# The tail between attention and the GELU stage rewritten: weight matrices on GpSimd's queue, some input rows loaded early, eight larger convolution steps

## The chip, the cores and the metric

The kernel runs on one core of one Trainium2 chip. The metric is the device time of one execution in microseconds (us), as a median of several runs. A profiled execution gives the trace, in which times are counted from the start of its span.

## What is computed

Two layers on an image batch of shape (4, 128, 128, 128): four images, 128 channels, 128 by 128 pixels, all in float32.

```python
# layer 0: windowed attention, then a feed-forward part with a 5x5 depthwise convolution
reg = windows of 16x16 pixels, step 14, so 9x9 per image        # neighbours share 2 rows/columns
tok = out_proj(attention(layernorm(reg))) + reg                 # 4 heads of 32
xf  = overlap-mean of the windows, back to the image
y   = layernorm(xf) @ w_p0 + b_p0                               # 128 -> 256 channels
ym  = depthwise_conv_5x5(y)                                     # 256 channels
ym  = batchnorm over (image, row, column) of ym
y   = gelu(gelu(ym)) @ w_p2 + b_p2 + xf
# layer 1: quantise to 4 bits, conv3x3, batchnorm, quantise, conv3x3, batchnorm, + identity
```

Two points matter here. The batch norm after the 5x5 convolution needs the mean and variance of every image, so no GELU can run before the last piece of the convolution is done. And a row of the convolution's output needs two rows of its input above and below it.

## The kernel before

**Bands.** Attention works in bands: `bands` lists 4 images times 9 rows of windows, 36 in all. In step t of the main loop the attention of band t runs, beside the layer norm of the bands to come, the post-processing of band t-1 and pieces of the convolution of bands long done. `beside(t)` returns these side steps and `run` carries them out; the order on TensorE, ScalarE, VectorE and SyncE is the order written in the program (`manual_schedule`). Each `normalise` ends in `spread`: a row of reciprocal deviations, stored by ScalarE's queue into `row`, is read back to all partitions as `xn`. Post-processing (`post_begin`, `post_chunks`) forms the seams of `ob` on GpSimd, multiplies with `wo` (L510), stores `xf`, normalises, multiplies with `wp0` (`p0`, L526; its result `y` is copied by ScalarE at L531) and stores `y` to `y2_d` in DRAM. A band's last `p0` steps are kept in the list `left` and run one band later.

**Convolution.** `y2_d` holds, per image, rows with two rows of padding above and below, columns split into even and odd. The convolution takes 16 output rows (`GR`) at a time: 20 input rows times two column parities are the 40 rows of the contraction (`KD`). For each channel a 40x32 matrix, three of them for the column shifts, is multiplied with 64 columns of each of `ng` row groups. Two channel halves and four channels run side by side in TensorE. The matrices lie in `dw_d`, built in the first band. `units` lists the pieces of the whole work: three whole images, then the last image in three parts: groups 0 to 3, groups 4 and 5, groups 6 and 7. The last part, `units[-1]`, reads rows up to the image's end and so can only be finished after the last band.

**The tail before.** After the main loop the band pools close (`bctx.close()`). Two pools are opened in their place (`tail`), with one buffer for the matrices and four for the rest. SyncE's queue issues the loads of the first four of eight matrix tiles `all_w`; then `run(beside(T))` does the last `left` steps and the post-processing of band 35; then `conv_steps(len(units) - 1, 4, ...)` runs sixteen steps of 8 channels a half. A step loads one input tile `u` four steps ahead (four DMAs: two halves, rows 0 to 15 and 16 to 19, 2 KB contiguous), multiplies (L611) into two `sc` tiles of PSUM in turn, copies both halves with ScalarE (L618), takes `bn_stats` on VectorE (L622), and puts four stores of 64 KB to `cv_d` on ScalarE's queue, in pieces of 256 bytes. The other four matrix tiles are loaded by SyncE's queue in the first four steps.

**After it.** 64 `bn_aggr` (L973), two small matmuls (L985) and `affine` (L913 to L919) give scale and shift. `gelu_stage` loads `cv` and `xfl` (L1099, L1104) and starts with image 0.

All DMAs of SyncE and ScalarE take turns on eight completion semaphores; each DMA waits until the one that used its semaphore before has landed.

Of the kernel before, what the change touches and what calls it, by code (L numbers as in the profile page):

```python
# [8 lines left out]
F32 = mybir.dt.float32  # L9
# [5 lines left out]
P = 128  # L15
# [5 lines left out]
NT = RS * RS  # L21
# [10 lines left out]
GR = 16  # L32
CW = P // 2
KD = 2 * (GR + 4)
NCK = 8
# [11 lines left out]
def layers(  # L47
# [127 lines left out]
    with ExitStack() as actx:  # L175
# [1 line left out]
            tc.tile_pool(name=f"{name}_{tag}", bufs=bufs, **k)  # L177
        )
        rp, op = pool("rp", 2), pool("op", 2)
        y2p, up, cp = pool("y2p", 1), pool("up", 3), pool("cp", 2)  # L180
        work, dev, xnp, xfp = pool("work", 1), pool("dev", 2), pool("xnp", 3), pool("xfp", 2)
        rowp = pool("rowp", 4, space=bass.MemoryType.DRAM)
        small = pool("small", 6)
# [3 lines left out]
        bctx = actx.enter_context(ExitStack())  # L187
        pool = lambda name, bufs: bctx.enter_context(tc.tile_pool(name=f"{name}_{tag}", bufs=bufs))
        xp, yp, sums = pool("xp", 2), pool("yp", 2), pool("sums", 1)
        att, attn_t, attn_v = pool("att", 2 if safe else 4), pool("attn_t", 2), pool("attn_v", 2)  # L190


# [203 lines left out]
        def flush(n, engine=nc.sync):  # L396
            for out, in_ in stores[:n]:
                engine.dma_start(out=out, in_=in_)
            del stores[:n]
# [149 lines left out]
        def weights(wt, k, jj, n, dma):  # L549
            for half in range(2):  # L550
                dma(
                    out=wt[64 * half : 64 * half + KD].rearrange("p s c m -> p s (c m)"),
                    in_=dw_d[2 * k + half, :, :, 256 * jj : 256 * (jj + n)],
                )

        def conv_steps(n, ahead=2, rest=None):

            b, g0, ng = units[n]  # L560
            nc_ = min(8, 32 // ng)
            tiles = [(k, jj, c) for k in range(NCK) for jj in range(2) for c in range(0, 8, nc_)]
            steps, U, W = [], {}, {}
            nj = nc_ // 4

            def load(at):
                k, jj, c = tiles[at]
                if rest:
                    W[k, jj] = rest[0][k][:, :, 8 * jj : 8 * jj + 8, :]
                    ut = rest[1].tile([P, ng * nc_ * CW], F32, name="u")  # L570
                else:
                    if c == 0:
                        W[k, jj] = up.tile([P, 3, 8, 32], F32, name="w")
                        weights(W[k, jj], k, jj, 1, nc.sync.dma_start)
                    ut = up.tile([P, 32 * CW], F32, name="u")[:, : ng * nc_ * CW]
                U[at] = ut = ut.rearrange("p (g c x) -> p g c x", g=ng, c=nc_)
                for half in range(2):
                    ch = 32 * k + 16 * half + 8 * jj + c
                    for a, z in ((0, GR), (GR, GR + 4)):
                        nc.sync.dma_start(  # L580
                            out=ut[64 * half + 2 * a : 64 * half + 2 * z].rearrange(
                                "p g c x -> p g (c x)"
                            ),
                            in_=bass.AP(
                                y2_d[b].tensor,
                                y2_d[b][GR * g0 + a, 0, ch, 0:1].offset,
                                [[2 * P * CW, 2 * (z - a)], [GR * 2 * 2 * P * CW, ng], [1, nc_ * CW]],
                            ),
                        )

            def products(at):
                k, jj, c0 = tiles[at]
                ut, wt = U.pop(at), W[k, jj]
                if rest:
                    sc = ps_s.tile([P, 2, 2, NT], F32, name=f"sc{at % 2}")
                    pc = [
                        sc[:, half].rearrange("p a n -> p (a n)")[:, : nj * ng * CW].rearrange(
                            "p (j g x) -> p j g x", j=nj, g=ng
                        )
                        for half in range(2)  # L600
                    ]
                else:
                    pc = [ps_m.tile([P, nj, ng, CW], F32, name="pm") for _ in range(2)]
                for j in range(nj):

                    for s, (a, z) in ((1, (0, CW)), (0, (1, CW)), (2, (0, CW - 1))):
                        for half in range(2):
                            hs = slice(64 * half, 64 * half + KD)
                            for q in range(4):
                                c = 4 * j + q  # L610
                                nc.tensor.matmul(  # L611
                                    pc[half][32 * q : 32 * q + 32, j, :, a:z],
                                    wt[hs, s, c0 + c, :], ut[hs, :, c, a + s - 1 : z + s - 1],
                                    start=(s == 1), stop=(s == 2),
                                )
                for half in range(2):
                    cv = (rest[1] if rest else cp).tile([P, nj, ng, CW], F32, name=f"c{half}")
                    nc.scalar.copy(  # L618
                        cv.rearrange("p j g x -> p (j g x)"), pc[half].rearrange("p j g x -> p (j g x)")
                    )  # L620
                    for j in range(nj):
                        nc.vector.bn_stats(  # L622
                            st0[:, k, half, 2 * jj + c0 // 4 + j, n, :], cv[:, j].rearrange("p g x -> p (g x)")
                        )
                        ch = 32 * k + 16 * half + 8 * jj + c0 + 4 * j
                        store(
                            bass.AP(
                                cv_d[b].tensor,
                                cv_d[b][g0, ch, 0:1].offset,
                                [[CW, P], [2 * P * GR * P, ng], [1, CW]],  # L630
                            ),
                            cv[:, j],
                        )

            def begin():
                for at in range(ahead):
                    load(at)

            steps.append(begin)
            for at in range(len(tiles)):  # L640
                def one(at=at):
                    if at + ahead < len(tiles):
                        load(at + ahead)
                    products(at)

                steps.append(one)
            return steps

        def attention(t):

# [199 lines left out]

        T = len(bands)
        todo, share, left, early = [], [0], [], []
        wq, kscale, tail = [], [], []
        one, two = quantised(0, w1), quantised(1, w2)
        for n in range(len(one) + 1):
            todo += one[n : n + 1] + two[max(n - 1, 0) : n]
# [10 lines left out]
        with nullcontext() if safe else tc.manual_schedule(engines=MANUAL):  # L867
            ln1_begin(0)
            for steps in zip(*ln1_chunks(0)):
                run(steps)  # L870
            last = None
            for t in range(T):
                flush(len(stores))
                scores, halves, values_in, values = attention(t)
                if t + 1 < T:
                    ln1_begin(t + 1)
                for j, side in enumerate(beside(t)):
                    scores(j)
                    if last:
                        last()  # L880
                    run(side[0])
                    halves(j)
                    if j == 0 and t:
                        post_begin(t - 1)
                    run(side[1])
                    if j % 2 == 0:
                        values_in(j)
                    run(side[2])
                    run(side[3])
                    last = lambda j=j, values=values: values(j)  # L890
            last()
            post_begin(T - 1)
            flush(len(stores))

            bctx.close()
            tail += [actx.enter_context(tc.tile_pool(name=f"late{n}_{tag}", bufs=n)) for n in (1, 4)]
            all_w = [tail[0].tile([P, 3, 16, 32], F32, name=f"w{k}") for k in range(NCK)]
            for k in range(NCK // 2):
                weights(all_w[k], k, 0, 2, nc.sync.dma_start)
            run(beside(T))  # L900
            flush(len(stores))
            run(todo)
            for n, s in enumerate(conv_steps(len(units) - 1, 4, (all_w, tail[1]))):
                s()
                flush(len(stores), nc.scalar)
                if n < NCK // 2:
                    weights(all_w[NCK // 2 + n], NCK // 2 + n, 0, 2, nc.sync.dma_start)
            flush(len(stores))

    def affine(mean, var, n, gamma, beta, name):  # L910

# [378 lines left out]
```

## Time and profile before

| | |
|---|---|
| median of 3 runs | 3295.52 us (3294.91 to 3316.36) |
| the profiled execution | 3291.11 us |
| its span | 3289.0 us |
| TensorE busy | 3093.5 us (94%) |
| VectorE, ScalarE, GpSimd busy | 2020.6 us, 1992.0 us, 828.3 us |
| DMA moved | 682.76 MB, mean 208 GB/s |
| DMA packets | 812363, of these under 512 bytes 581646 |

The span is what the profiler saw between first and last instruction; the time of the execution is 2.1 us longer. The page's second part cuts the span into 40 slices of 82.2 us, with busy shares in tenths. In later views "a <- b" with times means: a waited for b. PE is TensorE's matmul, PEld its weight load, DVE VectorE, ACT ScalarE, POOL GpSimd, SP SyncE; a q behind the name is the engine's queue of DMA issues. PEclk is the clock that TensorE was granted, 1.00 being full speed.

### The profile page before, as it was taken

To read this page: it belongs to the slowest core of one execution; us is meant where nothing else is said; L and a number is where in the kernel's file an instruction comes from. 1 tells how busy PE (TensorE), PEld (TensorE's weight loads), DVE (VectorE), ACT (ScalarE), POOL (GpSimd) and SP (SyncE) were. 2 spreads that over 40 slices of the span, in tenths; PEclk is the share of its full clock that TensorE was granted. 3 is DMA by queue.
4 is the path that set the end of the run, shared out by engine and by line. 5 is a ranking of instruction groups with operands and counts; after the bars stand their busy time and mean duration, and the time that the engine had idled before them with its cause. 6 is when DMAs were issued, how large, how long until landed. Compare 5 with 4: busy or idle time off the path is not lost.

```text
span 3289.0 us, 75777 instructions
## 1 busy us (share of the span) xinstructions
PE 3093.5 (94%) x30922; PEld 1541.3 (47%) x30922; DVE 2020.6 (61%) x3247; ACT 1992.0 (61%) x2670; POOL 828.3 (25%) x1042
## 2 busy tenths in 40 slices
PE   7999999999999999999998998884799999999998
PEld 4555554444544444544444444553444444444343
DVE  5777887776766667676555664542455555666543
ACT  5777776777777676777565564532477767333443
POOL 3444443333333333333222222210111111000000
PEclk9999999999999999999999998876699999999999
DMA  3455677888886788886899888766799999452298
GB/s 93 135 172 159 174 181 179 194 211 196 210 198 166 182 205 208 198 211 166 190 202 206 206 192 202 191 169 176 242 356 360 359 357 300 150 167 71 99 359 311
DMA packets 812363, 682.76 MB, mean 208 GB/s; under 512 B 581646, under 2 KB 696679, under 8 KB 812007
## 3 DMA queue, kind: packets, MB, share of 16 engines
q1 hardware_dynamic: 793447, 673.10, 74.8%
q10 hardware_dynamic: 18560, 4.72, 0.6%
q8 instruction: 247, 4.05, 0.5%
q14 instruction: 109, 0.89, 0.1%
HBM read 410.81 MB, written 270.81 MB: 207 GB/s over the span
## 4 chain that ended last, share of the span: by engine, by line
PE 77%; DMA 10%; ACT 5%; DVE 3%; SPq 2%; issue 2%; ACTq 0%; POOL 0%; DVEq 0%; POOLq 0%
PE pc L1064 19%; PE pm L611 9%; PE sc L684 9%; PE po L747 8%; PE pm L458 6%; PE pb L1122 6%; PE pm L526 5%; PE pm L670 4%; PE po L755 4%; DMA y_d<-y 3%; PE pm L510 3%; PE pm L357 3%; DMA xn<-row 2%; DMA cv_d<-c 2%; DMA u<-y_d 2%
## 5 line engine op out<-in xcount | busy, mean ns | idle before, releaser
L767 DVE RECIPROCAL rd<-po 128x256 f32<-128x256 f32 x324 | 569.3, 1757 | 451.2 <-PE po L755 448.3
L1064 PE MATMUL pc<-q,wq 128*128 128x512 fp8e4 x3168 | 702.0, 381 | 14.4 <-DVE q L1076 14.4
L692 ACT ACTIVATE pt<-sc 128x1024 f32<-128x1024 f32 x648 | 628.1, 1025 | 129.3 <-PE sc L684 65.1
L702 POOL TENSOR_TENSOR sm<-pt 128x512 f32<-128x512 f32 x324 | 412.9, 1274 | 1048.1 <-ACT pt L692 706.8
L1064 PEld LDWEIGHTS <-wq 128*128 128x128 fp8e4 x3168 | 309.0, 98 | 417.7 <-issue 50.2
L684 PE MATMUL sc<-q,kr 32*128 32x256 f32 x5184 | 405.1, 415 | 20.3 <-ACT pt L692 20.1
L611 PE MATMUL pm<-u,w 40*32 40x504 f32 (+5 forms) x7680 | 369.1, 504 | 33.8 <-DMA u<-y_d 20.8
L684 PEld LDWEIGHTS sc<-q,kr 32*128 32x128 f32 x5184 | 250.1, 190 | 259.3 <-issue 166.1
L747 PE MATMUL po<-pt,v 128*32 128x256 f32 x5184 | 361.5, 398 | 8.7 <-DVE part L771 7.7
L618 ACT COPY c<-pm 128x512 f32<-128x512 f32 (+1 forms) x256 | 132.0, 563 | 264.4 <-PE pm L611 254.4
L622 DVE BATCH_NORM_STATS2 st<-c 128x6 f32<-128x512 f32 (+2 forms) x384 | 174.6, 505 | 190.1 <-ACT c L618 189.5
L526 PE MATMUL pm<-xn,wp 128*128 128x512 f32 (+1 forms) x576 | 249.7, 565 | 37.2 <-ACT y L531 20.0
L531 ACT ACTIVATE y<-pm,bp 128x512 f32<-128x512 f32 (+1 forms) x288 | 183.0, 641 | 146.1 <-DMA y_d<-y 80.3
L458 PE MATMUL pm<-xn,wqkv 128*128 128x512 f32 (+1 forms) x576 | 251.5, 565 | 11.6 <-DVE xn L388 9.0
L702 DVE TENSOR_TENSOR sm<-pt 128x512 f32<-128x512 f32 x324 | 243.5, 751 | 29.7 <-ACT pt L692 29.5
L611 PEld LDWEIGHTS pm<-u,w 40*32 40x32 f32 x7680 | 145.2, 112 | 216.8 <-issue 161.4
L1122 PE MATMUL pb<-cv,wp 128*128 128x512 f32 x512 | 232.6, 598 | 11.4 <-ACT cv L1113 11.4
L747 PEld LDWEIGHTS po<-pt,v 128*32 128x32 f32 x5184 | 139.6, 111 | 182.7 <-issue 108.7
L1072 DVE BATCH_NORM_STATS2 st<-pc 128x6 f32<-128x512 f32 x256 | 165.6, 689 | 67.3 <-PE pc L1064 67.3
L755 PE MATMUL po<-sm,ones 128*32 128x256 f32 x2592 | 206.0, 390 | 0.0
L670 PE MATMUL pm<-wqkv,yr 128*128 128x128 f32 x1296 | 193.4, 290 | 0.0
L670 PEld LDWEIGHTS pm<-wqkv,yr 128*128 128x128 f32 x1296 | 159.0, 192 | 68.7 <-issue 44.4
(147 smaller groups left out, 3410.8 us busy)
## 6 DMA issues: line engine op xcount, KB each, us to landing
cv<-cv_d SPq DMA_DIRECT2D x64, 1024.0 KB
u<-y_d SPq DMA_DIRECT2D x224, 256.0 KB
cv_d<-c SPq DMA_DIRECT2D x192, 256.0 KB
xn<-row SPq DMA_DIRECT2D x80, 512.0 KB
y_d<-y SPq DMA_DIRECT2D x160, 256.0 KB
xfl<-xf_d SPq DMA_DIRECT2D x64, 512.0 KB
id_d<-y SPq DMA_DIRECT2D x64, 512.0 KB
idt<-id_d SPq DMA_DIRECT2D x64, 512.0 KB
```

Source lines behind the costliest of these rows:

```text
L458: nc.tensor.matmul(pm[:, : n * P], wqkv[:, m * P : (m + 1) * P], held["xn"][hh], start=True, stop=True,)
L526: nc.tensor.matmul(pm[:, : n * P], wp0[:, h, :], held["xn"][hh], start=True, stop=True)
L611: nc.tensor.matmul(pc[half][32 * q : 32 * q + 32, j, :, a:z], wt[hs, s, c0 + c, :], ut[hs, :, c, a + s - 1 : z + s - 1], start=(s == 1), s ...
L670: nc.tensor.matmul(pv[:, m, c, :], region(yr, j + m)[:, c * P : (c + 1) * P], wqkv[:, 2 * P :], start=True, stop=True,)
L684: nc.tensor.matmul(sc[h // 2][:, h % 2, kc, :].rearrange("p (r c) -> p r c", c=RS), region(kr, j)[hs, kc * P : (kc + 1) * P], queries(j, h ...
L692: nc.scalar.activation(pt, sc[p], AF.Exp)
L702: add(sm, pt[:, :, 0, :], pt[:, :, 1, :], ALU.add)
L747: nc.tensor.matmul(po[hs, 0, :], v[:, kc, hs], pt[h // 2][:, h % 2, kc, :], start=(kc == 0), stop=(kc == 1),)
L755: nc.tensor.matmul(po[hs, 1, :], ones, sm[h // 2][:, h % 2, :], start=True, stop=True)
L767: nc.vector.reciprocal(rd, po[:, 1, :])
L1064: nc.tensor.matmul(pc[:, h], w[:, t, :], q1[b][:, r + dy : r + dy + RB, dx : dx + P], start=(t == 0), stop=(t == 8),)
L1122: nc.tensor.matmul(pb[:, m], wp2[:, h, :], cv[:, h, px], start=(h == 0), stop=(h == 1))
```

## The change

Nothing changes in what is computed. The edits, in the order of the file:

- The pools `up` and `cp` (inputs, matrices and results of the convolution in the main loop) move into the band context `bctx`, so their memory is free after the loop.
- The inner loops of the convolution become a function `depthwise`, the address of an input a function `input_of`. `conv_steps` loses its second form for the tail.
- A new function `conv_rest` does the last part. It opens eight input tiles `u0` to `u7` (16 channels a half, 4 KB contiguous) and eight matrix tiles `w0` to `w7` at once. All 16 matrix loads go to GpSimd's queue. For the first five input tiles, rows 0 to 17 of the first row group (which come from earlier bands) are loaded before the last band's post-processing.
- The rest of the loads (`late`) comes after the post-processing: four steps ahead, then one further with each step. A step multiplies 16 channels a half into one `sc` tile, copies 128x512 per half, and stores each half with two DMAs of 128 KB: half 0 by SyncE's queue, half 1 by ScalarE's.
- The `left` steps of band 34 run before `conv_rest` is set up, not within `beside(T)`.

```diff
-        y2p, up, cp = pool("y2p", 1), pool("up", 3), pool("cp", 2)
+        y2p = pool("y2p", 1)
...
         xp, yp, sums = pool("xp", 2), pool("yp", 2), pool("sums", 1)
+        up, cp = pool("up", 3), pool("cp", 2)
...
+        def conv_rest(n, w_t, u_t, c_t):
+            b, g0, ng = units[n]
+            early = 5
+            at = GR + 2
+
+            def load(k, a, z, g, m):
+                for half in range(2):
+                    ch = 32 * k + 16 * half
+                    nc.sync.dma_start(
+                        out=U[k][64 * half + 2 * a : 64 * half + 2 * z, g : g + m].rearrange(
+                            "p g c x -> p g (c x)"
+                        ),
+                        in_=input_of(b, g0 + g, m, ch, 16, a, z),
+                    )
+
+            U = [u_t.tile([P, ng, 16, CW], F32, name=f"u{k}") for k in range(NCK)]
+            W = [w_t.tile([P, 3, 16, 32], F32, name=f"w{k}") for k in range(NCK)]
+            for k in range(NCK):
+                weights(W[k], k, 0, 2, nc.gpsimd.dma_start)
+            for k in range(early):
+                load(k, 0, at, 0, 1)
+
+            def late(k):
+                if k < early:
+                    load(k, 0, at, 1, 1)
+                    load(k, at, GR + 4, 0, ng)
+                else:
+                    load(k, 0, GR, 0, ng)
+                    load(k, GR, GR + 4, 0, ng)
+
+            def step(k):
+                sc = ps_s.tile([P, 2, 2, NT], F32, name=f"sc{k % 2}")
...
+                depthwise(pc, W[k], U[k], 16)
+                for half in range(2):
+                    cv = c_t.tile([P, 4, ng, CW], F32, name=f"c{half}")
+                    nc.scalar.copy(...)
+                    for j in range(4):
+                        nc.vector.bn_stats(...)
+                    engine = (nc.sync, nc.scalar)[half]
+                    for g in range(ng):
+                        engine.dma_start(...)
+
+            def run_all():
+                for k in range(4):
+                    late(k)
+                for k in range(NCK):
+                    step(k)
+                    if k + 4 < NCK:
+                        late(k + 4)
+            return run_all
...
             last()
+            assert not todo
+            flush(len(stores))
             post_begin(T - 1)
+            bctx.close()
+            pools = [actx.enter_context(tc.tile_pool(name=f"late{n}_{tag}", bufs=n)) for n in (1, 2)]
+            run(left)
+            left.clear()
             flush(len(stores))
-            bctx.close()
-            tail += [actx.enter_context(tc.tile_pool(name=f"late{n}_{tag}", bufs=n)) for n in (1, 4)]
-            all_w = [tail[0].tile([P, 3, 16, 32], F32, name=f"w{k}") for k in range(NCK)]
-            for k in range(NCK // 2):
-                weights(all_w[k], k, 0, 2, nc.sync.dma_start)
+            rest = conv_rest(len(units) - 1, pools[0], pools[0], pools[1])
             run(beside(T))
             flush(len(stores))
-            run(todo)
-            for n, s in enumerate(conv_steps(len(units) - 1, 4, (all_w, tail[1]))):
-                s()
-                flush(len(stores), nc.scalar)
-                if n < NCK // 2:
-                    weights(all_w[NCK // 2 + n], NCK // 2 + n, 0, 2, nc.sync.dma_start)
-            flush(len(stores))
+            rest()
```

## The prediction

> **What bounds the kernel now.** I read the page's slices first, then the windows of the place that stood out, then TensorE's timeline there, the waits, and the chain in order of time. The page's two TensorE rows show one deep gap:
>
> ```profile
> PE   7999999999999999999998998884799999999998
> PEclk9999999999999999999999998876699999999999
> ```
>
> A slice is 82.2 us. Slices 28 and 29 (2220 to 2384 us) have a busy share of 0.4 and 0.7 and the lowest clock. This is the tail the diff rewrites: the last band's post-processing, the last unit of the 5x5 convolution, its statistics, the start of the GELU stage. The rest of the span has TensorE at 0.8 to 0.9 and more and is not touched, so the whole effect must come from here. Windows, columns: stretch, length, busy PE, PEld, DVE, ACT, POOL, granted clock, DMA share, GB/s:
>
> ```profile
> 2219.00:2261.00 42.00, 18.18 (x80) 7.60 (x72) 10.00 (x20) 12.43 (x21) 1.78 (x4) 0.80 0.73 190
> 2261.00:2336.00 75.00, 48.72 (x1542) 41.13 (x1542) 27.91 (x139) 10.39 (x32) 0.00 (x0) 0.50 0.59 156
> 2336.00:2344.00 8.00, 2.13 (x8) 1.80 (x7) 2.30 (x17) 1.69 (x2) 4.54 (x13) 0.50 0.90 283
> 2310.00:2320.00 10.00, 8.75 (x304) 7.36 (x288) 4.86 (x24) 1.94 (x6) 0.00 (x0) 0.50 0.70 177
> ```
>
> No engine is full in the 75 us of the convolution: PE 0.65, DMA 0.59. The last row matters for later: 88% busy with these matmuls, and the clock stays at 0.50. The waits of 2215 to 2350 us (total, times, longest) say what is between the work:
>
> ```profile
> ACT c L618 <- DMA cv_d<-c: 35.1, 11, 6.0
> PE sc L611 <- DMA u<-y_d: 25.7, 13, 7.3
> SPq L580 <- DMA cv_d<-c: 19.5, 10, 5.2
> SPq L580 <- DMA u<-y_d: 17.4, 16, 2.6
> ```
>
> So latency binds: the queue may not issue the next input until earlier stores have landed, TensorE waits for inputs, ScalarE for its own stores. TensorE's timeline gives the price of the matmuls alone, and the chain gives the fixed points around them:
>
> ```profile
> 2264.45 7.45 PE L611 MATMUL sc<-u,w 40*32 40x128 f32 x271 [0.36 <-DMA u<-y_d]
> 2312.68 3.63 PE L611 MATMUL sc<-u,w 40*32 40x126 f32 x125 [0.39 <-issue]
> 2324.91 5.29 PE L611 MATMUL sc<-u,w 40*32 40x128 f32 x184 [1.03 <-DMA u<-y_d]
> ```
> ```profile
> 2232.46 3.68 DMA row<-rstd
> 2240.24 6.40 DMA xn<-row
> 2256.43 4.08 DMA y_d<-y
> 2261.75 2.56 DMA u<-y_d
> 2335.87 6.34 DMA xfl<-xf_d
> 2343.60 2.38 ACT cv L1110 x2
> ```
>
> Fixed points: xn has landed at 2246.6, TensorE starts the convolution at 2264.4 (17.8 later), ends it at 2330.2, the first GELU runs at 2343.6 (13.4 later).
>
> **What the Trainium skill says.** "DMA: Bandwidth & Descriptors", section "Issuing engines are not separate DMA queues": DMAs of all issuing engines interleave on the same 16 DMA engines, so another queue saves issue time only. The trace agrees in that SP spends 0.35 to 0.4 us on an issue that waits for nothing. Same page, "Anatomy of one DMA — SWDGE (gpsimd) path": a GpSimd DMA takes about 2.0 us plus bytes over 436 GB/s; for 240 KB that is an estimated 2.6 us from start to end; its "Specifications" give about 1 us to the first byte, against 0.6 on SP's path. The kernel before has no such DMA. "TensorE: Matmul & The Clock Gate", section "Part 1: The HAM clock gate": about 3.4 us of sustained matmuls lift the clock to full. The trace disagrees for these 40x32 tiles: 7.45 us without a gap from 2264.45, and 20 us at about 90% from 2300 on, leave it at 0.50. I follow the trace.
>
> **The change part by part.**
> *Main loop.* The pools up and cp only move to other addresses; buffers and order stay. The built program has every TensorE instruction in the old order. Cost 0.
>
> *Matrices by GpSimd.* Sixteen DMAs of 240 KB (3.84 MB) leave SP: the eight at 2224 to 2229.5 and eight between the input loads. GpSimd's last arithmetic ends at 2224.3, and nothing follows on it until the power in affine at 2337.7, so nobody queues behind these DMAs. They wait for the last cv_d stores of the loop (issued by 2224.2; with the 3.3 us that a store takes, landed about 2227.5). At an estimated 1 us of issue each (the first-byte price above, taken as work of GpSimd) they end about 2246; w0 is needed at about 2265. TensorE needs them later still for each step. Below zero they cannot go; at worst see rival D.
>
> *The old p0 steps first.* Four y_d stores that sat at 2236.2 on SP, behind the row write (2232.46 + 3.68), now go at about 2224.3. Then come the early input loads: ten of 144 KB. In the built program u0 to u2 can go at about 2229, but u3's first load waits for the completion semaphore that the row write holds (SP and ACT share eight). So u3 and u4 go after 2236.2, then both xf_d stores, then the two xn loads at about 2239.4 instead of 2240.2: 0.8 us gained. What lies ahead of xn in SP's ring shrinks from 0.77 MB of short pieces to 0.58 MB of long ones, but what is left of the matrices shares the DMA engines. If a third of the 3.84 MB is left, that is 1.3 MB at 360 GB/s = 3.6 us. Bounds -1.5 and +4; I take +1: xn at 2247.6. The next 17.8 us (normalise, p0, y_d stores, first loads; four loads before the first product, as before) stay: convolution from 2265.4.
>
> *Eight steps.* The matmuls are the same 1536 of 128 or 126 columns: (7.45+3.63)/(271+125) = 28.0 ns, with the third row 16.37/580 = 28.2 ns. At the cold clock 1536 x 28.5 = 43.8 us, 5.5 us a step; I keep 28.5 for the short starts. Inputs no longer wait for a free buffer: all eight tiles are open, and four steps are loaded ahead. Left in DMA: 144 KB of 4 KB lines twice plus 64 KB for u0 to u4, 640 KB for u5 to u7, and the same 4 MB of 256-byte stores, about 7.8 MB against 11.2 MB. At the 156 GB/s of the old window that is 50 us, but that window was not full (0.59): at the same rate per share, 29 us. DMA capacity is no bound; TensorE is. The semaphores still couple: u4's first load waits for the store of step 1's second half, u5's second load for that of step 2. With step 1 ending at 11 us, 1.8 for copies and issue, 4.5 for a store under load (the chain shows 1.7 to 4.8), 1.6 to issue four loads and 3 to land, u4 is there at about 22 us, when step 4 wants it. Bounds 0 and 14 us for all; I take 2. End: 2265.4 + 43.8 + 2 = 2311.2 instead of 2330.2. Beside it, per step, ACT 2 copies (about 0.6 us each) and 2 issues (1 us), DVE 8 statistics and 8 aggregates (3.4 us): covered by 5.5 us; uncovered, DVE's last ones are in the next sum.
>
> *To the first GELU.* Before: 13.4 us, because the first cv load waited for all stores of the tail (5.2 us after the end) and landed last. In the new program it waits for the last matmul and goes ahead of the last stores; 1 MB at the old 6.3 us is there when the statistics are. Those are late next: copies and first statistics 2.4 us, eight aggregates 1.7, then the 5.7 us from L975 (2333.69) to shift (2339.39): 9.8, say 9.9. First GELU at 2321.1 instead of 2343.6: 22.5 us. The stages after have the same instructions and only move.
>
> Sum: span 3289.0 - 22.5 = 3266.5; the profiled execution took 3291.1, so 3268.6; it lies 4.4 below the median 3295.5. On the median: 3273.
>
> **Rivals.**
> A, forecast: TensorE binds at half clock, 3262 to 3283. For it: the 0.50 at 88% busy.
> B, latency keeps binding: four late loads cost 3.5 us each, so 14 of 22.5 are lost: 3287. For it: the shared semaphores and stores of twice the size; against it: four steps of lead.
> C, dense matmuls do lift the clock: a step takes 3.3 us (the chain at 2148.06: 94 in 1.62, at full clock), the loads then bind at about 29 us for all, 17 less: 3256. For it: the skill; against it: two long cold stretches.
> D, GpSimd's DMAs are slow. With g us each the last matrix is there at 2229.5 + 16g, then a step and 9.9. From g = 4.8 it binds, from g = 6.2 (2245 + 99 = 2344) the kernel is slower than before; at 8.5 the first GELU is at 2381, 3333. For it: no such DMA in the trace; against it: 2.6 us by the skill.
> That the early loads aren't early is partly so already (u3, u4) and is in A.
>
> **How the numbers follow.** A 0.66, B 0.16, C 0.11, D 0.07. About 1% (33 us) is what a measurement of this kernel can tell from no change. A and B lie within it: 0.82; C faster 0.11; D slower 0.07. The range holds A and B: 3262 to 3290.
>
> **What would show it.** Right: in the profile after, some 1536 matmuls on sc without gaps over 1 us for about 44 to 47 us, clock 0.50, starting about 2265; the first cv load issued at their end, not 5 us later; the first GELU bound by the shift. Wrong: waits of TensorE for u (B), a clock of 1.00 there (C), waits for w (D), or xn later than 2251.

## The result, and the profile after

The changed kernel took 3291.28 us (median of 11 runs, 3286.86 to 3299.39) against 3306.11 us for the kernel before beside it (11 runs, 3294.91 to 3316.36): ratio 0.9963, 95% interval 0.9949 to 0.9978. A second comparison on another chip gave 3289.77 against 3304.60, ratio 0.9955 (0.9939 to 0.9970). So it is faster, but only by about 0.4%; the forecast was 0.68% (22.5 of 3295.5), and 3291.28 lies above the range's end of 3290. The profiled execution took 3289.4 us, its span 3287.5.

The two TensorE rows of the page and the line of GpSimd's queue (packets, MB, share of 16 engines):

```profile
PE   7999999999999999999999998884899999999998
...
PEclk8999999999999999999999998876699999999999
...
q0 software_dynamic: 1024, 3.93, 0.5%
```

The gap in slices 28 and 29 is narrower at its end but as deep at its start. The windows, at stretches of before and at three of 7 us where the row write and xn are under way (columns as above):

```profile
2219.00:2261.00 42.00, 15.78 (x270) 7.85 (x268) 10.18 (x25) 10.57 (x20) 10.73 (x21) 0.77 0.88 218
2261.00:2336.00 75.00, 53.76 (x1552) 42.87 (x1552) 25.27 (x122) 14.08 (x24) 0.00 (x0) 0.55 0.61 155
2240.00:2247.00 7.00, 0.00 (x0) 0.00 (x0) 0.00 (x0) 0.82 (x2) 1.96 (x5) 0.61 0.85 205
2247.00:2254.00 7.00, 0.00 (x0) 0.00 (x0) 0.00 (x0) 0.00 (x0) 1.79 (x4) 0.50 0.94 261
2254.00:2261.00 7.00, 0.00 (x0) 0.00 (x0) 0.00 (x0) 0.00 (x0) 0.00 (x0) 0.50 0.94 266
2310.00:2320.00 10.00, 8.79 (x318) 7.72 (x318) 5.84 (x31) 1.98 (x4) 0.00 (x0) 0.50 0.97 241
```

The DMA share ahead of the convolution has risen from 0.73 to 0.88, and from 2247 on it is 0.94 with TensorE, VectorE and ScalarE all idle. That is the new place where the time goes. The waits of 2215 to 2350 us (total, times, longest):

```profile
DVE xn L389 <- DMA xn<-row: 27.4, 1, 27.4
...
POOL w L552 <- DMA w<-dw_d: 10.0, 8, 1.6
PE sc L566 <- DMA u<-y_d: 8.3, 1, 8.3
...
ACT c L686 <- DMA cv_d<-c: 5.2, 1, 5.2
...
PE sc L566 <- issue: 4.4, 5, 1.7
...
ACT cv L1171 <- DVE shift L980: 1.8, 1, 1.8
```

TensorE's wait for inputs is down from 25.7 us in 13 pieces to 8.3 in one (ahead of the first product), ScalarE's wait for its stores from 35.1 to 5.2. In their place stands one wait of 27.4 us for `xn`, which was 14.3 before:

```profile
DVE xn L388 <- DMA xn<-row: 14.3, 1, 14.3
```

TensorE's timeline shows the convolution running through:

```profile
2267.46 9.48 PE L527 MATMUL pm<-xn,wp 128*128 128x512 f32 x16 [29.41 <-DVE xn L389]
2285.28 15.50 PE L566 MATMUL sc<-u,w 40*32 40x128 f32 x534 [8.35 <-DMA u<-y_d]
2301.17 3.67 PE L566 MATMUL sc<-u,w 40*32 40x128 f32 x126 [0.39 <-issue]
2306.57 7.26 PE L566 MATMUL sc<-u,w 40*32 40x126 f32 x255 [1.73 <-issue]
2315.04 7.25 PE L566 MATMUL sc<-u,w 40*32 40x128 f32 x253 [1.21 <-issue]
2322.85 7.38 PE L566 MATMUL sc<-u,w 40*32 40x126 f32 x254 [0.56 <-issue]
2330.77 3.53 PE L566 MATMUL sc<-u,w 40*32 40x126 f32 x114 [0.54 <-issue]
```

From the queues' timelines, GpSimd's matrices, and SyncE's issues up to xn:

```profile
2234.24 4.27 POOL L552 DMA_DIRECT2D w<-dw_d  x8 [3.04 <-DMA y_d<-y]
2239.71 0.51 POOL L552 DMA_DIRECT2D w<-dw_d  x1 [1.19 <-DMA w<-dw_d]
...
2252.08 0.51 POOL L552 DMA_DIRECT2D w<-dw_d  x1 [1.26 <-DMA w<-dw_d]
```
```profile
2236.39 12.40 SPq L655 DMA_DIRECT2D u<-y_d  x10
2248.89 1.30 SPq L399 DMA_DIRECT2D xf_d<-xf  x2
2251.68 2.21 SPq L380 DMA_DIRECT2D xn<-row  x2
```

The waits of SyncE's own queue on the way to xn, one row of before and two of after:

```profile
SPq L398 <- DMA row<-rstd: 6.6, 1, 6.6
...
SPq L655 <- DMA row<-rstd: 8.5, 1, 8.5
SPq L380 <- DMA u<-y_d: 3.0, 2, 1.6
```

**Where the time went.** The last attention product ends at different times in different profiles, so I count from it: R is the end of the last attention sums product (2219.83 in the profile of before, L755; 2226.74 after, now L820). In every profile here but two the row write is issued at R+12.6; in those two it is 13.1 and 13.9.

| us | forecast | before, two profiles | after, two profiles |
|---|---|---|---|
| xn landed, from R | 27.8 | 26.8, 28.3 | 40.0, 42.0 |
| then to the first product | 17.8 | 16.8, 17.3 | 18.6, 18.6 |
| convolution | 45.8 | 66.8, 69.3 | 49.0, 47.9 |
| end to first GELU | 9.9 | 13.4, 13.8 | 9.1, 9.1 |
| first GELU, from R | 101.3 | 123.8, 128.7 | 116.7, 117.6 |
| first GELU to the end | 945.4 | 945.4, 943.9 | 944.1, 944.9 |

The convolution gives back about 20 us, as forecast, and the end 4.5 (forecast 3.5); 13 to 14 of them are paid beforehand, while xn is on its way, and 1.5 more between xn and the first product.

### The profile page after: what moved, and what is told of

The parts are those of the page before. It is cut to its first block, busy times and chain, and to the rows that moved or that the text cites. A ratio compares the mean times of both kernels' runs of the same rounds, so it can differ in the third digit from the quotient of the medians.

```text
span 3287.5 us, 75680 instructions
## 1 busy us (share of the span) xinstructions
PE 3089.1 (94%) x30922; PEld 1540.7 (47%) x30922; DVE 2018.0 (61%) x3247; ACT 1989.9 (61%) x2654; POOL 836.3 (25%) x1058
## 3 DMA queue, kind: packets, MB, share of 16 engines
q0 software_dynamic: 1024, 3.93, 0.5%
## 4 chain that ended last, share of the span: by engine, by line
PE 76%; DMA 9%; ACT 5%; issue 4%; DVE 3%; SPq 2%; POOL 0%; ACTq 0%; DVEq 0%; POOLq 0%
PE pc L1125 19%; PE pm L566 9%; PE sc L749 9%; PE po L812 8%; PE pm L459 7%; PE pb L1183 6%; PE pm L527 5%; PE pm L735 4%; PE po L820 3%; DMA y_d<-y 3%; PE pm L358 3%; PE pm L511 3%; DMA u<-y_d 2%; ACT pt L757 1%; DMA xn<-row 1%
## 5 line engine op out<-in xcount | busy, mean ns | idle before, releaser
L1125 PE MATMUL pc<-q,wq 128*128 128x512 fp8e4 x3168 | 701.4, 381 | 14.3 <-DVE q L1137 14.3
L566 PE MATMUL pm<-u,w 40*32 40x504 f32 (+5 forms) x7680 | 369.2, 504 | 37.2 <-DMA u<-y_d 24.9
L767 DVE TENSOR_TENSOR sm<-pt 128x512 f32<-128x512 f32 x324 | 243.3, 751 | 27.4 <-ACT pt L757 27.4
L617 DVE BATCH_NORM_STATS2 st<-c 128x6 f32<-128x512 f32 (+2 forms) x320 | 160.8, 550 | 138.5 <-ACT c L613 137.9
L1133 DVE BATCH_NORM_STATS2 st<-pc 128x6 f32<-128x512 f32 x256 | 165.6, 689 | 66.8 <-PE pc L1125 66.8
L820 PE MATMUL po<-sm,ones 128*32 128x256 f32 x2592 | 205.7, 388 | 0.0
```

The costliest lines, as they stand in the source:

```text
L566: nc.tensor.matmul(outs[half][32 * q : 32 * q + 32, j, :, a:z], wt[hs, s, c, :], ut[hs, :, c, a + s - 1 : z + s - 1], start=(s == 1), stop ...
L767: add(sm, pt[:, :, 0, :], pt[:, :, 1, :], ALU.add)
L820: nc.tensor.matmul(po[hs, 1, :], ones, sm[h // 2][:, h % 2, :], start=True, stop=True)
L1125: nc.tensor.matmul(pc[:, h], w[:, t, :], q1[b][:, r + dy : r + dy + RB, dx : dx + P], start=(t == 0), stop=(t == 8),)
```

## The experiments

Two theories. **Sharing**: the matrices and the early rows fill the DMA engines just when the 4 KB row write and the 1 MB of xn, on which everything hangs, must pass. **Path**: GpSimd's queue itself is what delays (the prediction's rival D in a milder form). Beside these, the moved pools might change the main loop.

**No early rows.**

```diff
-            early = 5
+            early = 0
```

> Edit: early = 0, so no input row is loaded before the last band's post-processing; all else as in the changed kernel. Times below count from the end of the last sums product of attention; there xn landed at 26.7 us before and 40.0 us after the change, and the first GELU ran at 123.7 and 116.7 us. Theory W (the matrices that GpSimd's queue moves in the same stretch delay the row write and xn): xn still late, at 34 to 38 us, first GELU at 112 to 116. Theory U (the early input rows, queued on SP ahead of xn, delay it): xn back at 26 to 29 us, first GELU at 103 to 107.

Measured: 3283.19 us, ratio 0.9928 (0.9900 to 0.9956). xn landed at R+31.8, the convolution took 53.0 us, the first GELU came at R+114.0. xn lies between the two forecasts, the first GELU in that of theory W. The row write still lands late, 7.7 us after its issue where it took 3.7 before; SyncE's queue, which has no early loads now, waits for it:

```profile
SPq L380 <- DMA row<-rstd: 9.3, 1, 9.3
```

The matrices alone cost xn 5.0 us (31.8 - 26.8). The late row write adds nothing to that, because SyncE has nothing left to issue between it and xn: xn is issued at R+20.3, as before (20.4). The 5.0 us lie in xn's own read, 11.5 us instead of 6.4. Of the other 8.2 the early rows are a necessary part.

**The matrices after xn.** A small copy on GpSimd reads xn, and the matrix tiles depend on it.

```diff
-            for k in range(NCK):
-                weights(W[k], k, 0, 2, nc.gpsimd.dma_start)
+            def matrices(src):
+                g = small.tile([P, NCK], F32, name="gate", bufs=1)
+                nc.gpsimd.tensor_copy(g, src[:, :NCK])
+                for k in range(NCK):
+                    nc.gpsimd.tensor_copy(W[k][:, 0, 0, 0:1], g[:, k : k + 1])
+                    weights(W[k], k, 0, 2, nc.gpsimd.dma_start)
...
-            run(beside(T))
+            steps = beside(T)
+            run(steps[:12])
+            matrices(spreads[-1])
+            run(steps[12:])
```

> Edit: GpSimd copies eight numbers of the second xn tile into the matrix tiles before it issues their loads, so that the matrices start when xn has landed; the early input rows stay where they are. Theory W: xn back at 26 to 30 us after the last sums product (40.0 in the changed kernel); the matrices then meet the y_d stores, so the convolution starts 19 to 24 us after xn instead of 18.5, first GELU at 106 to 112 us. Theory U: xn stays at 36 us or later, first GELU at 115 to 122.

Measured: 3299.48 us, ratio 0.9984 (0.9972 to 0.9996). xn lands at R+26.1: the early rows alone cost it nothing. But the matrices now run beside the last y_d stores (SyncE's timeline, then TensorE's wait):

```profile
2262.43 22.91 SPq L400 DMA_DIRECT2D y_d<-y  x8
```
```profile
PE sc L567 <- DMA u<-y_d: 22.5, 1, 22.5
```

Eight stores that took 8.5 us to issue take 22.9, and the convolution starts 32.5 us after xn instead of 18.6 (I had expected 19 to 24). The 13.9 us saved are the 13.9 us lost. The delay belongs to the matrices' traffic, and follows it to what is critical next.

**The matrices by SyncE's queue, same place.**

```diff
-                weights(W[k], k, 0, 2, nc.gpsimd.dma_start)
+                weights(W[k], k, 0, 2, nc.sync.dma_start)
```

> Edit: the same sixteen matrix loads at the same place of the program, but on SP's queue instead of GpSimd's. If the number of bytes in front of xn is what counts (theory W in its plain form), xn is as late or later, 40 to 48 us after the last sums product, because SP's loads, which wait for each other's semaphores, now also hold up the early rows and the xf_d stores behind them. If GpSimd's way of issuing DMAs is itself what slows the stretch, xn is back at 30 us or earlier.

Measured: 3294.89 us, ratio 0.9969 (0.9956 to 0.9982); xn at R+44.0, later than by GpSimd. SyncE's timeline:

```profile
2236.32 15.86 SPq L552 DMA_DIRECT2D w<-dw_d  x16
2253.29 10.21 SPq L655 DMA_DIRECT2D u<-y_d  x10
...
2265.14 2.03 SPq L380 DMA_DIRECT2D xn<-row  x2
```

This weakens Path without settling it. The row write is late without GpSimd's queue too: it lands 6.5 us after its issue (3.7 before, 7.9 in the changed kernel). But xn is late here for a reason of its own. On SyncE's queue the 16 issues and their waits stand ahead of xn's issue, which comes 37.5 us after R instead of 24.9; by then the matrices have landed, and xn's read takes 6.5 us, as before. So no run shows the same matrices beside xn's read by a queue other than GpSimd's. What was seen fits the Trainium skill, "DMA: Bandwidth & Descriptors", section "Issuing engines are not separate DMA queues", which the prediction named: another queue relieves the issuing engine, here by 12.6 us, and not the DMA engines, for beside GpSimd's matrices xn's read takes 15.0 us.

**The moved pools alone, in the kernel before.**

```diff
-        y2p, up, cp = pool("y2p", 1), pool("up", 3), pool("cp", 2)
+        y2p = pool("y2p", 1)
...
+        up, cp = pool("up", 3), pool("cp", 2)
```

> Edit: the kernel before, with only the pools up and cp moved into the band context; the tail is the old one. The measured ratio of the change is 0.9963 (some 12 us) while its profiled tail is only 7 us shorter. If the other 5 us are scatter of the main loop: ratio to before 1.000 within 0.0015. If the new addresses of the convolution's tiles in the main loop save them: ratio 0.998 to 0.999.

Measured: 3298.39 us (22 runs), ratio 0.9981 (0.9971 to 0.9992). The first GELU comes at R+123.6, as in the first profile of before (123.8), so the 6 us, if they are of the pools, do not show in this tail; I return to this below.

**Half of the matrices late.** `w0` to `w3` stay; `w4` to `w7` wait for the last rows of `u0`.

```diff
-            for k in range(NCK):
+            for k in range(NCK // 2):
                 weights(W[k], k, 0, 2, nc.gpsimd.dma_start)
...
+                for k in range(NCK // 2, NCK):
+                    for half in range(2):
+                        hs = slice(64 * half, 64 * half + KD)
+                        nc.gpsimd.tensor_copy(W[k][hs, 0, 0, 0:1], U[0][hs, 1, 0, k : k + 1])
+                    weights(W[k], k, 0, 2, nc.gpsimd.dma_start)
```

> Edit: matrices w0 to w3 go by GpSimd's queue as in the changed kernel; w4 to w7 wait, by small GpSimd copies from u0 into them, until u0's late rows have landed. Early rows as they are. Counted from the last sums product of attention. If the amount that shares the DMA engines between attention and xn decides (5.3 MB in the changed kernel, 3.4 MB here, 1.9 MB before): xn at 27 to 31 us, convolution from 44 to 49, 47 to 50 us long, first GELU at 101 to 107 (changed kernel 116.7), ratio to before 0.991 to 0.994. If any matrices beside the early rows spoil it: xn at 36 or later, first GELU 112 or later.

Measured: 3291.68 us, ratio 0.9950 (0.9932 to 0.9969); xn at R+32.6. Half the bytes take away 7.4 of the 13.2 us, which again lies between the two forecasts; the first GELU, at R+113.4, does not come early. xn's own read is back at 6.5 us. What is left is seen in SyncE's timeline: xn is issued late, because the early rows stand ahead of it and among them is a wait for the row write.

```profile
2234.76 18.10 SPq L655 DMA_DIRECT2D u<-y_d  x10
2252.97 1.21 SPq L399 DMA_DIRECT2D xf_d<-xf  x2
2254.23 2.07 SPq L380 DMA_DIRECT2D xn<-row  x2
```

and from the waits of SyncE's queue there:

```profile
SPq L655 <- DMA row<-rstd: 13.5, 2, 12.8
```

**The same, with the early rows issued behind xn.** The first 12 side steps end with the xn loads.

```diff
-            for k in range(early):
-                load(k, 0, at, 0, 1)
+            def ahead():
+                for k in range(early):
+                    load(k, 0, at, 0, 1)
...
-            run(beside(T))
+            steps = beside(T)
+            run(steps[:12])
+            flush(len(stores))
+            ahead()
+            run(steps[12:])
```

> Edit: as e5_half_late, and the early rows are queued on SP behind the two xn loads instead of ahead of them. If the order on SP counts beside the amount: xn at 25 to 27 us, y_d stores delayed by 1 to 3 us, convolution from 43 to 47, first GELU at 100 to 104, 1 to 3 us better than e5_half_late. If only the amount counts: xn as in e5_half_late within 1 us and the first GELU equal or later.

Measured: 3279.45 us, ratio 0.9923 (0.9904 to 0.9941), below both kernels. xn at R+27.1, first GELU at R+106.9: 16.9 us earlier than in the first profile of before, 9.8 earlier than in that of the changed kernel. The order counts beside the amount, and by more than I had expected: 6.5 us against the kernel with half of the matrices late, not 1 to 3.

```profile
2241.27 1.88 SPq L380 DMA_DIRECT2D xn<-row  x2
2243.26 7.25 SPq L655 DMA_DIRECT2D u<-y_d  x10
2251.29 8.79 SPq L399 DMA_DIRECT2D y_d<-y  x8
```

The rows are still early enough: they are issued by 2250.5, before p0's first y_d store is due, and its eight stores take 8.8 us to issue (8.5 in the changed kernel). From the chain of waits of this kernel:

```profile
2233.68 7.58 DMA row<-rstd
...
2241.27 6.42 DMA xn<-row
```

xn's own read is back at the 6.4 us of before. The row write still takes 7.6, with half of the matrices about; it costs nothing more here, since xn is issued at R+20.7 where it was R+20.4.

**The same bytes in another shape.** The matrices after xn as above, and at the old place sixteen loads of the same bytes spread over all 128 partitions instead of 40; the matrices are thus loaded twice.

```diff
+            for k in range(NCK):
+                for half in range(2):
+                    nc.gpsimd.dma_start(
+                        out=W[k].rearrange("p s c m -> p (s c m)")[:, 480 * half : 480 * half + 480],
+                        in_=dw_d[2 * k + half].rearrange("p s n -> (p s n)").rearrange("(p n) -> p n", p=P),
+                    )
```

> Edit: as e2_w_after_xn, but at the place where the changed kernel loads the matrices GpSimd issues sixteen loads of the same bytes of dw_d spread over 128 partitions (128x480) into the matrix tiles, which are loaded again, rightly, after xn. If the number of bytes delays xn: xn at 38 to 42 us after the last sums product, as in the changed kernel. If it is the shape, 6 KB rows for only 40 partitions a load, the wide loads are done in 11 to 14 us and xn is at 27 to 32. The time as a whole is of no interest here: 3.9 MB are moved twice.

Measured: one run of 3319.42 us; for xn, the number wanted here, R+33.2, between the two forecasts. Without early matrices it is 26.1, with them in their own shape 40.0, so the same bytes in the wide shape cost about half of the 13.9 us. By the packets of GpSimd's queue 3.93 MB took 27 us in the changed kernel (R+10.1 to R+37.4) and 20 us in this shape (R+7.9 to R+28.3). But this does not make the other half the price of the shape. The wide loads also began 2.2 us earlier. And the same loads into 40 partitions took no more than 18 us in the kernel with the matrices after xn, and 20 us in the second set of this run, both beside y_d stores. So what else moves at the time counts too. The Trainium skill, "SBUF — State Buffer", section "Door 1: The DMA port swizzle", says that a transfer's rate depends on how many of SBUF's 16 ports its partitions reach; partitions 0 to 39 reach 8 by its formula. The 20 against 27 us would fit that, but every second load goes to partitions 64 to 103, which by the formula reach the other 8 ports, several loads are under way at once, and the packets' length changed too. Whether the shape costs anything of its own is not shown.

**Half late, no early rows.** As "half of the matrices late", with `early = 0`.

> Edit: as e5_half_late with early = 0. If the early rows are worth loading once the matrices are thinned out: xn at 26 to 27 us, convolution 51 to 55 us long as in e1_no_early (53.0), first GELU at 104 to 108, later than e5_half_late by 1 to 5. If they are worth nothing: first GELU equal or earlier than in e5_half_late.

Measured: 3284.99 us, ratio 0.9931 (0.9908 to 0.9954). xn at R+26.8, as before the change; the convolution takes 58.8 us, longer than expected, instead of 50.4. So beside late matrices the early rows are worth 8.4 us in the convolution, and issued behind xn they cost it nothing (first GELU 115.3 without them, 106.9 with them). Ahead of xn and beside all the matrices they cost more than they are worth (116.7 with them, 114.0 without). How they shorten the convolution is not shown: the trace has the 8.4 us as gaps of "issue" (time in which TensorE waits for nothing that the profile shows; 12.7 us against 3.5), not as waits for `u` (10.5 against 10.8).

**Four second profiles.** How far do single profiles carry? The same programs again, on another chip.

> The changed kernel unaltered, a second profile. Times from R, the end of the last attention sums product. Theory 'sharing': the tail is fixed by what lies in its queues, so it repeats within 1 us: xn landed at R+40, convolution 58.5 to 107.6, first GELU at R+116.7, while R itself (2226.7 before) may fall anywhere between 2219 and 2245; ratio 0.995 to 0.998. Rival 'chance': the late landing of the row write and of xn was one execution's bad luck; then xn lands at R+27 to R+32 here and the first GELU comes at R+104 to R+109.

> The kernel before unaltered, a second profile. Theory 'sharing': first GELU again at R+123.8 within 1 us, ratio 1.000 with an interval of 0.2%. R: if it is fixed by the program (theory 'program'), 2219.8 within 1 us; if it scatters from execution to execution (theory 'execution'), several us off.

> The changed kernel with no early rows, a second profile. Its first ratio, 0.9928, is 13 us better than its tail's 9.8 us explain. Theory 'program': this repeats, with 0.992 to 0.994 and R within 1 us of 2225.5. Theory 'execution': the surplus is scatter of the main loop; the ratio moves to 0.995 to 0.997 and R by several us. The first GELU stays at R+114.0 within 1 us in both.

> Early rows behind the xn loads and half of the matrices behind the last rows, again. Theory 'sharing': xn at R+27, first GELU at R+107 within 1 us, so 10 us earlier than in the changed kernel on the same chip; ratio 0.990 to 0.994, below that of the changed kernel with intervals apart. Rival 'chance': first GELU at R+112 or later, or intervals that overlap with the changed kernel's.

| | R | xn | first GELU | median us | ratio |
|---|---|---|---|---|---|
| after | 2223.3 | 42.0 | 117.6 | 3289.77 | 0.9955 (0.9939 to 0.9970) |
| before | 2232.3 | 28.3 | 128.7 | 3305.86 | 1.0001 (0.9990 to 1.0012) |
| no early rows | 2225.4 | 30.7 | 111.1 | 3285.98 | 0.9948 (0.9931 to 0.9965) |
| rows after xn, half late | 2222.4 | 28.9 | 110.1 | 3280.65 | 0.9934 (0.9917 to 0.9951) |

That the late xn was one execution's bad luck is excluded: the delay is there again. The rows 2236.33 and 2244.10 of the last kernel's chain show the same two transfers:

```profile
2236.33 7.75 DMA row<-rstd
...
2244.10 7.20 DMA xn<-row
```

The reordered kernel is 9.1 us below the changed one on this chip (3280.65 against 3289.77; six runs of 3276.1 to 3287.1, nine of 3280.3 to 3298.1). But the intervals against before overlap by 0.0012, which I had named as a sign of chance here; in the first comparisons, 0.9923 against 0.9963, they lie apart. In the tail it is 7.5 us earlier this time, not 9.8. And my "within 1 us" was too strict: the first GELU repeats within 0.9, 5.0, 2.9 and 3.2 us, and R of the kernel before moved by 12.5 us. A single profile shows a mechanism of 10 us in the tail well; it does not show 3 us, and nothing at all can be read from R.

**What stays open.** With the means over the two profiles, the tail explains 9.1 us of the changed kernel's gain (126.25 - 117.15), and the two ratios ask for 12.2 and 14.9. For the reordered kernel it is 17.8 against 25 and 22, without early rows 13.7 against 24 and 17. Some 3 to 10 us are left over. The pools moved alone gave 6, of which the tail (123.6 against 126.25) explains 3, which would fit the lower end; but the kernel with the matrices after xn, whose pools are moved too, gained 8.9 in the tail and only 5.3 in all. Whether new addresses help the main loop by a few us, or what else does, is not settled. Nor is what exactly the row write and xn wait for inside the DMA engines, and whether matrices by SyncE's queue beside xn's read would slow it as much.

## Why the prediction was right and wrong

**The step that failed** is "what is left of the matrices shares the DMA engines ... Bounds -1.5 and +4; I take +1". It was +13.2 (+12.2 on the forecast, of 15.4 for the whole tail). xn later than 2251, R+31.2, was one of the prediction's own signs of being wrong, and it is the one that came. Both halves of the term were mis-sized:

- *What the rest costs.* I had the matrices end at about 2246, that is R+26, at 1 us of issue each. Issue took 0.5 us, but from the ninth on each waited for the one eight before it to land (10.0 us in 8 waits), and the last bytes came at R+37.4. Not the issue set the pace but the transfer: about 145 GB/s, the engines shared with the early rows and xn. When the row write was issued (R+12.6) 3.4 of the 3.9 MB were left. When xn was (R+24.9) it was 1.7 MB, not far from the 1.3 assumed; but they ran on for 12 us, not 3.6.
- *What it meets.* I charged the leftover only against xn's 1 MB. The row write, 4 KB that took 3.68 us from issue to landing, now took 7.9, and SyncE's queue went on at R+20.5 instead of R+16.3. I had left it at 3.68, and had even noted that `u3`, `u4`, and so xf_d and xn behind them, wait for its semaphore. Then came the four loads of `u3` and `u4`, both xf_d stores and a wait of 1.5 us for an early load that held xn's semaphore. So xn was issued at R+24.9 instead of R+20.4, and then took 15.0 us instead of 6.4: 4.5 + 8.6, the 13.2 within rounding.

All the profiles agree on both. The row write took 1.6 to 5.0 us in the four without the new matrix loads ahead of xn, and 6.0 to 9.2 in the ten with them. xn's read took 6.4 to 7.5 us in the nine where no matrices ran on for more than 5 us after its issue, and 10.2 to 17.5 in the five where they did. The DMA packets in the first profiles of before and after show that the small write waits in line rather than moves slowly: its packets of 1 KB take about 0.1 us or less in both, but the first comes 6.2 us after the issue instead of 2.2.

**The early rows "instead" of short y_d pieces** I had taken as a gain of 0.8 us for xn. By themselves they cost nothing (R+26.1); beside the matrices they cost 8.2 (40.0 - 31.8; in the second profiles 11.3). I priced two loads on one resource one at a time.

**The eight steps**: right in kind. The products took 44.6 us (forecast 43.8), the clock stayed at 0.50 (rival C is out), and after the first product the trace shows no wait for an input (rival B's 14 us are out). The stalls were 4.4 us against 2, and of another kind: gaps of "issue", not waits for `u`. They cost 0.4 to 1.7 us each, and what fills them is not shown; since they grow to 8.6 us without early rows, waits for inputs that the profile does not show are possible.

**To the first GELU**: 9.1 against 9.9. The first cv load was issued at the convolution's end (2334.33), and the shift released the GELU, as said.

**xn to the first product**: 18.6 against 17.8. The first product of before was at 2263.4, so that the true stretch there was 16.8; the row I quoted was the second piece.

**Rival D**: its price (g of 4.8 or more) is far off; a matrix DMA took 27/16 = 1.7 us of the stream, though each landed only 13.0 us (median) after its issue, where the prediction had estimated 2.6 for one alone. No product waited for `w`.

**The base.** I wrote 3295.5 as the median to reckon from, of three runs; with more runs it is 3304 to 3307. And the profile I reckoned in had the shorter tail of the two (123.8 and 128.7). Of the 18.3 us between the forecast of 3273 and 3291.28, 10.6 are the base (3306.1 - 3295.5), and only 7.7 a missing gain. The gain in the ratio is free of the base, and it was half to two thirds of the forecast. That it was so much is luck: the tail gave 9.1 of 22.5, and 3 to 6 us came from somewhere that the prediction had put at nothing. The same holds for the nearness of rival B's 3287, whose mechanism did not occur, and in part for the reordered kernel's 0.9923 and 0.9934, close to what the prediction had forecast for the change (1 - 22.5/3295.5 = 0.9932), of which its tail gives 17.8 us.

## What to carry to other kernels

When loads are moved to "an idle time" of another queue, ask what small, latency-bound transfer must pass through the DMA engines just then: here 4 KB and 1 MB on the critical chain lost 13 us to 5.4 MB (3.93 of matrices, ten loads of 144 KB) that no product needed for some 30 us after the row write. Price transfers that will run together by their sum and by the window's remaining DMA share, not one at a time; then order them by who is needed first, xn, then the rows, then the matrices in two parts, which turned a gain of 9 us in the tail into 18. And check a single profile's tail against a second one before working out differences of less than 5 us.

## What I had not expected of the hardware

- GpSimd issues a DMA of 240 KB in 0.5 us, eight in a row in 4.27 us; then it waits for landings.
- Sixteen such loads into 40 partitions each moved 3.93 MB in 27 us beside early rows and xn, and in 18 us beside y_d stores; over 128 partitions the same bytes took 20 us beside early rows and xn.
- A 4 KB store took 3.7 and 5.0 us in the two profiles of before, with the DMA engines at 0.37 and 0.53, and 7.6 to 7.9 in the changed kernel and the reordered one, with them at 0.86 and 0.95.
- In the Trainium skill, "TensorE: Matmul & The Clock Gate", section "Part 1: The HAM clock gate" has a few us of sustained matmuls lift the clock. The 49 us of convolution, 44.6 of them busy, stayed at 0.50; the measurement decides, for these 40x32 tiles. For the 128x128 products of p0 just before it, the same trace agrees with the page: 0.50 from 2267.5 to 2272.0, 0.98 from there to 2277.0.
